# An attention and expert block on one core: the last sequence's experts computed densely, and score stacks of 128 rows

## The chip, the cores and the metric

The kernel runs on one core of a Trainium2 chip. The metric is device time in microseconds (us) of one execution. A core has a matrix engine (PE, with its weight loads as PEld), a vector engine (DVE), an activation engine (ACT), a general engine (POOL) and an engine that here only issues transfers (SP). Each works through its own queue of instructions in order and waits on semaphores for the others. SBUF is the on-chip memory of 128 partitions, PSUM the memory that PE writes to, DRAM the memory outside.

## What is computed

`x` is 8 sequences of 256 tokens with 128 channels, f32. Four residual steps follow each other, each on the LayerNorm of `x`:

```python
x = x + attn_a(layernorm(x))     # 16 heads of 8 channels; w_qkv and w_proj in 8 groups of 16 channels
x = x + ffn(layernorm(x))        # f = 0
x = x + attn_b(layernorm(x))     # 16 heads of 8; dense Wq, Wk, Wv, Wo; q and k RMS-normalised per head
x = x + ffn(layernorm(x))        # f = 1, the same weights as f = 0

def ffn(h):                      # 16 experts, each token goes to its best 4
    probs = softmax(h @ router_w + router_b)
    topw, topi = top_k(probs, 4)
    topw = topw / sum(topw)
    combine = sum(one_hot(topi, 16) * topw[..., None], axis=2)
    out = 0
    for e in range(16):          # 128 -> 256 -> 128
        hmid = gelu(h @ w1[e] + b1[e], approximate=False)
        out = out + (hmid @ w2[e] + b2[e]) * combine[:, e, None]
    return out
```

## The kernel before

**Tiles.** The 2048 tokens are 16 tiles of 128 (`NT`), two to a sequence, and two halves `hf` of 8 tiles (`TPH`). `x` stays in SBUF as `x_sb` for the whole kernel.

**Attention** (`attention`, scores in L734 to L758, weighing in L760 to L782). A sequence is four steps (`SEQ`); a step does four heads twice. q and k are split into three bf16 parts (`split2`, `split_cast`, `split3`, L502 to L529), written to DRAM (`qd`, `kd`) and read back by `stack_in` (L531 to L543) as stacks `qst` and `kst` of 128 partitions x 16 heads x 256 tokens, of which 72 rows are filled (R = 9 x 8: nine products of the parts). They come from a pool with two buffers per tag. One scores matmul (L745) takes 72 rows, 128 keys and 256 queries; ACT takes the exponential of 1024 columns at once (L754); the weighing of the values (L772) uses 32 columns of PE per head. The first sequence of attention a goes another way, in f32 (`project_1`, `scores_1`), with its `q1` and `k1` in the buffers of the stacks.

**Experts** (`routed`, `experts`, `fetched`). For each half, `route1` to `route3`, `chosen`, `rows_of` pick each token's 4 experts and give it a row in each expert's room of CAP = 320 rows; the row numbers come from a matmul in `route2`. `send` (L952) scatters each tile's rows into `sent[hf]` in DRAM: POOL issues 4 indirect DMAs per tile (L959). Then the 16 experts run in pairs, one expert a step: `load` (L1008) reads a pair's rows, `turn` (L1021) transposes them, `front` (L1037) does the first matmul into `ps_h` (L1045) and the gelu (L1053), `second` (L1061) the second into `ps_y` (L1068); DVE adds the bias into `ys` (L1075) and the ACT queue stores it to `made[hf]` (L1083). `fetch` (L1107) gathers each token's 4 results back, 4 indirect DMAs per tile on POOL (L1118); `combine` (L1125) adds them to `x_sb` with their weights (four DVE operations per tile, L1129) and, for f = 1, writes the tile out (L1136). The first two of a tile's 4 results (`EARLY`) are read from the rows of the first 14 experts alone, so that their gathers need not wait for the last pair; they are placed at the half's end - 0.5, the others at the end + 1.5. For the first half four tiles are fetched at first and the other four as buffers come free; in the last half of f = 1 all eight are fetched at once, into two tiles `yg4` in the buffers of `kst`.

**Order.** The order on PE, ACT, DVE and SP is written out by hand: main units (attention steps and expert steps) are numbered 0 to END - 1, each is a front and a back one step later, and every other piece is put at a place between them with `at(place, f)`. The places are the tables FINISH, ROUTE, PREPARE, COMBINE, PROJECT, TURN and BACK (L55 to L92), in steps from the sequence's or half's own step. `needs` and `done` check at build time that a piece stands behind what it builds on. POOL's order follows from the order in which the pieces are reached. The units run in this order:

```python
units = attention(0, wo_a, ga, 1, base[0])
for hf in range(NH):
    units += experts(0, hf, base[1] + hf * E)
units += attention(1, wo_b, gb, 3, base[2])
for hf in range(NH):
    units += experts(1, hf, base[3] + hf * E)
```

A buffer is reused when its last reader is done: PSUM has three buffers for transposes and small results (`ps_tr`), one for `ps_acc` (`ps_y` and `ps_av`) and two for the big ones (`ps_big`).

Of the kernel before, what the change touches and what calls it, by code (L numbers as in the profile page):

```python
# [40 lines left out]
P = 128  # L42
# [8 lines left out]

FINISH = [[[1.5, 1.7, 2.5, 3.5, 3.7], [-0.5, 0.1, 1.9, 2.9, 3.1], [0.7, 0.9, 2.1, 2.3, 2.3]],  # L55
          [[0.7, 2.1, 2.5, 3.9, 3.9], [0.3, 0.3, 2.7, 3.7, 3.7], [0.7, 0.9, 1.7, 2.7, 2.9]]]

ROUTE = [[[[4.7, 4.7, 5.7, 6.9, 6.9, 7.1, 7.7, 10.1], [5.5, 5.5, 6.5, 6.9, 6.9, 7.9, 7.9, 11.7],
           [4.5, 4.9, 4.9, 5.9, 6.1, 6.7, 6.7, 9.1]],
          [[5.3, 5.3, 5.9, 5.9, 5.9, 9.9, 9.9, 9.9], [6.7, 6.7, 7.7, 8.7, 8.9, 9.3, 9.3, 10.3],  # L60
           [4.1, 4.1, 5.1, 5.3, 5.3, 7.9, 8.3, 9.1], [3.5, 3.5, 4.5, 5.5, 5.7, 6.3, 6.3, 7.3]]],
         [[[4.3, 5.3, 6.5, 7.3, 7.5, 7.5, 7.5, 9.5], [4.5, 5.7, 6.1, 6.7, 6.7, 7.7, 7.9, 11.7],
           [4.3, 4.5, 5.5, 6.5, 6.7, 7.5, 7.7, 8.7]],
          [[5.5, 5.7, 6.5, 6.7, 7.7, 9.1, 9.3, 10.5], [4.5, 4.5, 5.5, 6.3, 6.3, 6.7, 6.7, 9.7],
           [4.5, 4.9, 5.5, 6.1, 6.1, 7.9, 7.9, 8.7], [3.1, 3.7, 4.7, 5.3, 6.1, 6.9, 7.1, 9.1]]]]

PREPARE = [[-7.97, -7.96, -7.95, -6.9, -5.9, -5.9, -5.9, -5.9, -3.9],
           [-11.5, -10.5, -9.5, -9.5, -7.9, -7.9, -7.9, -7.9, -6.9],
           [-11.1, -10.1, -9.1, -8.7, -7.7, -7.5, -6.3, -6.3, -6.3],
           [-12.5, -11.5, -10.5, -9.9, -7.7, -7.300000000000001, -5.5, -5.5, -4.5],  # L70
           [-11.7, -10.7, -9.7, -8.9, -7.9, -7.9, -7.9, -7.9, -6.9],
           [-13.3, -12.3, -11.3, -11.3, -9.9, -8.7, -7.9, -7.9, -6.5]]

COMBINE = [[[5.1, 5.5, 6.5, 7.5, 9.5, 11.5, 13.7, 15.5],
            [5.9, 5.9, 6.9, 7.9, 9.9, 12.1, 14.1, 16.1]],
           [[8.9, 6.9, 9.9, 11.9, 12.9, 14.9, 15.9, 17.9],
            [4.5, 5.5, 6.5, 6.5, 8.5, 11.5, 14.5, 15.5]]]

PROJECT = [[[6.7, 7.3, 8.1, 8.5, 9.3, 9.7, 9.7, 9.7, 11.1],
            [8.3, 9.3, 10.3, 11.1, 11.1, 12.1, 13.1, 13.1, 13.5],  # L80
            [13.1, 14.1, 15.1, 16.1, 16.1, 17.1, 18.1, 18.1, 19.1],
            [16.5, 18.7, 19.3, 19.3, 20.5, 21.3, 22.7, 22.7, 23.9]],
           [[6.3, 6.7, 8.5, 8.5, 10.1, 10.3, 11.3, 11.3, 11.7],
            [8.7, 9.5, 10.5, 10.5, 11.5, 12.5, 14.1, 14.1, 15.5],
            [13.5, 13.5, 14.5, 14.5, 15.5, 16.5, 17.5, 17.5, 18.5],
            [16.5, 17.5, 18.5, 18.5, 19.3, 20.9, 21.1, 21.1, 22.1]]]
# [9 lines left out]
def fast_path(  # L96
# [38 lines left out]
    RJ = CAP // HP  # L135
# [6 lines left out]
    LIMITS = [(E - 2) * CAP] * EARLY + [E * CAP] * (TOPK - EARLY)  # L142
# [150 lines left out]
    first_i = const.tile([P, E], I32, name="first_i")  # L293
    nc.gpsimd.iota(first_i, pattern=[[-CAP, E]], base=TOP, channel_multiplier=0)
    first = const.tile([P, E], F32, name="first")
    nc.gpsimd.tensor_copy(first, first_i)
# [7 lines left out]

    limit = const.tile([P, TOPK], F32, name="limit")
    for c, rows in enumerate(LIMITS):
        nc.gpsimd.memset(limit[:, c : c + 1], float(TOP - rows + 1))
# [4 lines left out]
    b2_bc = const.tile([P, NPAIR, C], F32, name="b2_bc")  # L312

# [39 lines left out]
    def load_b2():  # L353
        b2p = b2.rearrange("(r a) c -> a r c", a=2)
        for a in range(2):
            nc.sync.dma_start(
                b2_bc[a * HP : (a + 1) * HP], b2p[a : a + 1].to_broadcast((HP, NPAIR, C))
            )
# [105 lines left out]
    class Group:  # L464


        def __init__(self, t0, t1):
            self.t0, self.t1, self.n = t0, t1, t1 - t0
            self.step = None

# [21 lines left out]
    def ln_transpose(g, rows=None):  # L492
        pt = ps_tr("pt_h")
        for i in range(g.n):
            row = g.h[:, i, :] if rows is None else rows[:, g.t0 + i, :]
            nc.tensor.transpose(pt[:, i * P : (i + 1) * P], row, ident)  # L496
        hT = work.tile([P, g.n * P], F32, tag=f"hT{g.n}", name="hT")
        nc.scalar.copy(hT, pt[:, : g.n * P])  # L498
        g.hT = hT


# [29 lines left out]
    def stack_in(g, queue=nc.sync, parts=1, part=0):  # L531

        qd, kd = g.qkd
        if part == 0:
            g.qst = work.tile([P, H, N], BF16, tag="qst", name="qst")
            g.kst = work.tile([P, H, N], BF16, tag="kst", name="kst")
# [15 lines left out]
    def project_1(g):  # L552
# [4 lines left out]
        g.q1 = work.tile([P, NJ, N], F32, tag="qst", name="q1")  # L557
        g.k1 = work.tile([P, N], F32, tag="kst", name="k1")
# [4 lines left out]
    def heads_1(g, j0, j1):  # L563
        for j in range(j0, j1):
            nc.vector.tensor_scalar(g.q1[:, j, :], g.pq1, one_head[:, j : j + 1], None, ALU.mult)
# [127 lines left out]
    between = {}  # L693
    done = set()
# [9 lines left out]
    def attention(which, w_out, groups, k_next, base):  # L704
# [4 lines left out]
        def scores_1(n):  # L709
# [5 lines left out]
            for i in range(4):  # L715
# [3 lines left out]
                    g.q1[32 * i : 32 * i + 32, 2 * hf : 2 * hf + 2, :].rearrange("p j n -> p (j n)"),  # L719
# [14 lines left out]
        def scores(n):  # L734
# [4 lines left out]
            exs[n] = []  # L739
            for u in range(2):  # L740
                ps = ps_big("ps_st")
                for hh in range(2):
                    h = (hf * 4 + 2 * u + hh) * 2 + jj
                    for c in range(TB):
                        nc.tensor.matmul(  # L745
                            ps[:, hh, c * N : (c + 1) * N],
                            kst[0:R, h, c * P : (c + 1) * P],
                            qst[0:R, h, :],
# [146 lines left out]
    def route2(g, earlier, exps):  # L895
# [6 lines left out]
        g.exps = exps  # L902
        ps = ps_tr("ps_row")
# [16 lines left out]
    def rows_of(f, g):  # L920

        hf = g.t0 // TPH
        r3 = g.rows.rearrange("p (t e) -> p t e", e=E)
        here = work.tile([P, g.n, E], F32, tag=f"here{g.n}", name="here")
        nc.vector.scalar_tensor_tensor(here, r3, float(CAP), g.mb, ALU.is_lt, ALU.mult)
        key = work.tile([P, g.n, E], F32, tag=f"key{g.n}", name="key")
        nc.vector.tensor_tensor(
            key, first.unsqueeze(1).to_broadcast([P, g.n, E]), r3, ALU.subtract
# [12 lines left out]
        if g.t1 % TPH == 0:  # L941
            nc.vector.tensor_tensor(here, r3, g.mb, ALU.add)
            nc.vector.tensor_reduce(
                most[:, f * NH + hf : f * NH + hf + 1],
                here.rearrange("p t e -> p (t e)"),
                AX.X,
                ALU.max,
            )
# [24 lines left out]

    def route3(f, g):
# [4 lines left out]
            g.tk, g.tk, limit.unsqueeze(1).to_broadcast([P, g.n, TOPK]), ALU.max  # L979
        )  # L980
        if not g.exps:
            t = work.tile([P, g.n, E], F32, tag=f"exl1{g.n}", name="ex1", bufs=1)
            nc.vector.tensor_scalar(t, g.ex, -1.0, 1.0, ALU.mult, ALU.add)
            nc.vector.reciprocal(t, t)
            nc.vector.scalar_tensor_tensor(g.ex, g.ex, 1.0, t, ALU.add, ALU.mult)
# [17 lines left out]
    def experts(f, hf, base):  # L1003

        xs, hs, gs, ys = {}, {}, {}, {}
        JA = 3

        def load(r):  # L1008
            if r == 0:
                assert len(scattered[hf]) == TPH * TOPK  # L1010
            x = work.tile([P, RJ, C], F32, tag="xs", name="xs", bufs=3)
            ins = nc.sync.dma_start(
                x, sent[hf][r * 2 * CAP : (r + 1) * 2 * CAP].rearrange("(p j) c -> p j c", j=RJ)
# [7 lines left out]
        def turn(r, part):  # L1021
            if part == 0:
                hs[r] = work.tile([P, 2, RJ, HP], F32, tag="hs", name="hs")
# [13 lines left out]
        def front(e):  # L1037
# [5 lines left out]
            g = work.tile([P, NI, RJ, HP], F32, tag="ex", name="g", bufs=4)  # L1043
            for n in range(NI):
                nc.tensor.matmul(  # L1045
                    ps[:, n, :CAP],
                    w1_sb[r][:, a, n * P : (n + 1) * P],
                    hs[r][:, a].rearrange("p j q -> p (j q)"),
# [3 lines left out]
            for n in range(NI):  # L1052
                nc.scalar.activation(  # L1053
                    g[:, n].rearrange("p j q -> p (j q)"),
                    ps[:, n, :CAP],
# [5 lines left out]
        def second(r, j0, j1):  # L1061
            if j0 == 0:
                ys[r] = work.tile([P, RJ, C], F32, tag="ys", name="ys")
# [17 lines left out]
            if j1 == RJ:  # L1081
                del gs[2 * r], gs[2 * r + 1]
                nc.scalar.dma_start(  # L1083
                    made[hf][r * 2 * CAP : (r + 1) * 2 * CAP].rearrange("(p j) c -> p j c", j=RJ),
# [17 lines left out]

    yg = {}
# [3 lines left out]
    def fetch(f, t, c0, c1, last=False):  # L1107

        needs(("fetchable", f, t))
        if last:  # L1110
            i = t % 4
            if i == 0:
                many.append(work.tile([P, 4, TOPK, C], F32, tag="kst", name="yg4"))
# [3 lines left out]
        for c in range(c0, c1):  # L1117
# [3 lines left out]
                in_=made[t // TPH][0 : LIMITS[c]],  # L1121
# [18 lines left out]
    END = base[3] + NH * E  # L1140
# [14 lines left out]

# [734 lines left out]
```

## Time and profile before

| | us |
|---|---|
| runs | 683.42, 679.70, 676.77, 677.83; median 678.77 |
| profiled execution | 682.4, span 680.6, mean granted PE clock 0.787 |
| attention a, about | 0 to 150 |
| experts f = 0 | 150 to 312 |
| attention b | 312 to 490 |
| experts f = 1 | 490 to 634 |
| last gathers and combines | 634 to 680.6 |

| engine | busy us | share of the span |
|---|---|---|
| PE | 470.3 | 69% |
| ACT | 281.8 | 41% |
| DVE | 267.1 | 39% |
| POOL | 260.0 | 38% |

The profile is one execution. A group row reads: line, engine, operation, output<-input, shape and count, then busy time and mean ns of one, then the idle time of the engine just before these instructions and what ended most of it. "remote" or "another core or an unknown queue" is a wait whose end the profile could not tie to an instruction. The granted clock is the share of full speed that PE was given. In the page's slices each digit is a tenth of a slice of 17 us. A row of windows gives busy time and count of instructions of each engine in a stretch, then the clock, the busy share of the DMA engines and GB/s.

### The profile page before, as it was taken

Reading aid. Unit: us, or ns where it says so; the run is one execution under the profiler, and the core shown is the slowest. Engines: PE = TensorE matmul, PEld = TensorE weight load, DVE = VectorE, ACT = ScalarE, POOL = GpSimd, SP = SyncE. Lnnn points to the kernel's source line nnn. Section 1 sums busy time; section 2 is a strip of 40 time slices with the busy share of each in tenths; the row PEclk is TensorE's granted clock in tenths of the full one; section 3 lists DMA queues with packets and bytes.
Section 4 is the critical chain, followed back from the end, with each engine's and each line's share of the span. In section 5 each row is a group of like instructions: output and inputs, shape, how many; then the busy total and the mean of one; then the engine's idle time right before and its main releaser. Section 6 shows DMA issues by size and latency. Waiting matters only on the chain.

```text
span 680.6 us, 10365 instructions
## 1 busy us (share of the span) xinstructions
PE 470.3 (69%) x3739; PEld 297.2 (44%) x3739; DVE 267.1 (39%) x1086; ACT 281.8 (41%) x523; POOL 260.0 (38%) x303
## 2 busy tenths in 40 slices
PE   7799559788787938787673976786739795896100
PEld 3366334355455716454241553343527463564100
DVE  5346333335541103484172673442427311042323
ACT  5589325465232403355372762564613242342000
POOL 6100724404453263504444007053533506235674
PEclk9899865777787978798595877686859888697655
DMA  4777742745443423247164163352113233332322
GB/s 114 185 181 212 193 113 82 177 130 154 149 127 105 127 70 99 78 122 190 45 152 99 38 146 104 78 134 88 55 46 99 101 121 96 97 94 86 92 59 59
DMA packets 53283, 76.53 MB, mean 112 GB/s; under 512 B 9032, under 2 KB 36200, under 8 KB 51064
## 3 DMA queue, kind: packets, MB, share of 16 engines
q1 hardware_dynamic: 40104, 48.41, 26.9%
q0 software_dynamic: 8224, 16.86, 9.0%
q10 hardware_dynamic: 4896, 10.52, 4.1%
q8 instruction: 31, 0.51, 0.3%
q14 instruction: 28, 0.23, 0.1%
HBM read 42.73 MB, written 33.03 MB: 111 GB/s over the span
## 4 chain that ended last, share of the span: by engine, by line
PE 48%; another core or an unknown queue 19%; ACT 9%; DVE 8%; issue 8%; DMA 4%; POOL 2%; SPq 1%; DVEq 0%; ACTq 0%; POOLq 0%
PE ps_y L1068 11%; PE ps_h L1045 9%; PE ps_av L772 8%; PE ps_st L745 7%; ACT ex L754 5%; PE pt_x L1028 4%; PE pq L618 2%; DVE x_sb L1129 2%; POOL yg L1118 2%; DVE ys L1075 2%; PE pp L829 1%; PE ps_lg L860 1%; PE pt_o L790 1%; DMA kst<-kd 1%
## 5 line engine op out<-in xcount | busy, mean ns | idle before, releaser
L959 POOL DMA_INDIRECT sent<-h,dst x128 | 123.5, 965 | 199.8 <-DVE dst L938 95.9
L1118 POOL DMA_INDIRECT yg<-made,src x128 | 121.4, 949 | 163.5 <-issue 56.6
L754 ACT ACTIVATE ex<-ps_st 128x1024 f32<-128x1024 f32 x120 | 117.1, 1023 | 66.9 <-PE ps_st L745 35.5
L1068 PE MATMUL ps_y<-w_sb,g 128*64 128x128 f32 x1280 | 94.4, 299 | 48.6 <-DVE ys L1075 41.4
L1068 PEld LDWEIGHTS ps_y<-w_sb,g 128*64 128x64 f32 x1280 | 77.7, 150 | 80.3 <-DVE ys L1075 51.0
L772 PE MATMUL ps_av<-ex,vst 128*32 128x256 f32 x1024 | 96.9, 456 | 17.6 <-ACT av L782 8.5
L745 PE MATMUL ps_st<-qst,kst 72*128 72x256 bf16 x480 | 77.2, 309 | 30.8 <-issue 22.1
L1045 PE MATMUL ps_h<-hs,w_sb 128*128 128x320 f32 x256 | 96.3, 503 | 2.6 <-issue 1.9
L1075 DVE TENSOR_TENSOR ys<-ps_y,b_bc 128x384 f32<-128x384 f32 x64 | 31.4, 490 | 165.5 <-remote 69.2
L1053 ACT ACTIVATE g<-ps_h,b1T 128x320 f32<-128x320 f32 x128 | 60.7, 526 | 61.8 <-PE ps_h L1045 36.4
L745 PEld LDWEIGHTS <-kst 72*128 72x128 bf16 x480 | 51.5, 110 | 51.2 <-issue 39.4
L1029 ACT COPY hs<-pt_x 128x384 f32<-128x384 f32 x64 | 26.9, 427 | 100.7 <-PE pt_x L1028 23.4
L1045 PEld LDWEIGHTS ps_h<-hs,w_sb 128*128 128x128 f32 x256 | 50.9, 221 | 18.4 <-issue 9.8
L772 PEld LDWEIGHTS ps_av<-ex,vst 128*32 128x32 f32 x1024 | 32.1, 122 | 60.4 <-issue 42.1
L1129 DVE SCALAR_TENSOR_TENSOR x_sb<-yg,wgt,x_sb 128x128 f32<-128x128 f32 x128 | 44.3, 352 | 30.7 <-DMA yg<-made,src 23.3
L1028 PE MATMUL pt_x<-ident,xs 128*128 128x128 f32 x160 | 33.6, 316 | 2.2 <-issue 2.2
L841 DVE TENSOR_TENSOR x_sb<-pp,x_sb 128x256 f32<-128x256 f32 x16 | 6.8, 422 | 51.5 <-remote 30.8
L498 ACT COPY hT<-pt_h 128x256 f32<-128x256 f32 (+1 forms) x30 | 11.7, 388 | 36.2 <-PE pt_h L496 14.9
L600 POOL TENSOR_TENSOR x_sb<-x_sb,bp_bc 128x256 f32<-128x256 f32 x8 | 6.2, 778 | 49.0 <-DVE h L483 49.0
L1028 PEld LDWEIGHTS pt_x<-ident,xs 128*128 128x128 f32 x160 | 19.9, 156 | 10.8 <-issue 9.9
L790 PE MATMUL pt_o<-ident,av 128*128 128x128 f32 x64 | 13.1, 339 | 12.5 <-ACT av L782 12.5
L860 PE MATMUL ps_lg<-rw_sb,hT 128*128 128x16 f32 x64 | 11.8, 306 | 13.3 <-ACT hT L498 9.8
(159 smaller groups left out, 464.9 us busy)
## 6 DMA issues: line engine op xcount, KB each, us to landing
xs<-sent SPq DMA_DIRECT2D x32, 320.0 KB
made<-ys ACTq DMA_DIRECT2D x32, 320.0 KB
qst<-qd SPq DMA_DIRECT2D x45, 192.0 KB
kst<-kd SPq DMA_DIRECT2D x45, 192.0 KB
sent<-zero SPq DMA_DIRECT2D x20, 256.0 KB
w_sb<-in_L_ffn_w_dram SPq DMA_DIRECT2D x16, 256.0 KB
qd<-qk_parts SPq DMA_DIRECT2D x15, 192.0 KB
kd<-qk_parts SPq DMA_DIRECT2D x15, 192.0 KB
```

Of the source, the lines that this page charges most:

```text
L745: nc.tensor.matmul(ps[:, hh, c * N : (c + 1) * N], kst[0:R, h, c * P : (c + 1) * P], qst[0:R, h, :], start=True, stop=True,)
L754: nc.scalar.activation(ex, ps.rearrange("p h (c n) -> p h c n", c=TB), AF.Exp, scale=SCALE)
L772: nc.tensor.matmul(acc[32 * i : 32 * i + 32, hf * N : (hf + 1) * N], groups[b].v[:, c, v0 : v0 + W], ex[i // 2][:, i % 2, m, :], start=(jj ...
L959: ins = nc.gpsimd.indirect_dma_start(out=sent[hf], out_offset=bass.IndirectOffsetOnAxis(ap=dst[:, g.t0 + i, c : c + 1], axis=0), in_=g.h[: ...
L1028: nc.tensor.transpose(pt[:, (j - j0) * P : (j - j0 + 1) * P], x[:, j, :], ident)
L1029: nc.scalar.copy(hs[r][:, :, j0:j1, :], pt[:, : (j1 - j0) * P].rearrange("p (j a q) -> p a j q", a=2, q=HP),)
L1045: nc.tensor.matmul(ps[:, n, :CAP], w1_sb[r][:, a, n * P : (n + 1) * P], hs[r][:, a].rearrange("p j q -> p (j q)"), start=True, stop=True,)
L1053: nc.scalar.activation(g[:, n].rearrange("p j q -> p (j q)"), ps[:, n, :CAP], AF.Gelu, bias=b1T[:, e * NI + n : e * NI + n + 1],)
L1068: nc.tensor.matmul(acc[a * HP : (a + 1) * HP, (j - j0) * C : (j - j0 + 1) * C], gs[2 * r + a][:, n, j, :], w2_sb[r][:, a, n, :], start=(n ...
L1075: nc.vector.tensor_tensor(ys[r][:, j0:j1, :], acc[:, : (j1 - j0) * C].rearrange("p (j c) -> p j c", c=C), b2_bc[:, r, :].unsqueeze(1).to_b ...
L1118: nc.gpsimd.indirect_dma_start(out=yg[t][:, c, :], out_offset=None, in_=made[t // TPH][0 : LIMITS[c]], in_offset=bass.IndirectOffsetOnAxis ...
L1129: nc.vector.scalar_tensor_tensor(x, y[:, c, :], wgt[:, t, c : c + 1], x, ALU.mult, ALU.add)
```

## The change

1. In f = 1, the last sequence (two tiles) is neither sent nor gathered. Its routing stops after the choice of the experts; `weights_of_all` makes a weight for each of the 16 experts (zero for those not chosen). Sixteen steps behind the sparse ones (`all_experts`) run each expert on all 256 tokens of the sequence, and DVE adds each result to `x_sb` with its column of weights; the biases come in with one small matmul. POOL then issues 8 scatters and 8 gathers fewer, and the last half has CAP3 = 256 rows per expert and 6 tiles.
2. The stacks `qst` and `kst` are four fixed tiles in two pairs, used in turn. POOL clears their rows 64 to 127 at the start, and scores matmuls go over all 128 rows; the rows behind the 72 are zero. `q1` and `k1` of the first sequence lie in the room of the first expert weights, and the last gathers in the two tiles `qst`.
3. The tables of places are new, FINISH, ROUTE, PREPARE, COMBINE and PROJECT; of them the diff below shows parts.

The diff, cut to its core:

```diff
+CAP3 = 256
...
-          [[5.5, 5.7, 6.5, 6.7, 7.7, 9.1, 9.3, 10.5], [4.5, 4.5, 5.5, 6.3, 6.3, 6.7, 6.7, 9.7],
-           [4.5, 4.9, 5.5, 6.1, 6.1, 7.9, 7.9, 8.7], [3.1, 3.7, 4.7, 5.3, 6.1, 6.9, 7.1, 9.1]]]]
+          [[5.5, 5.7, 6.5, 6.7, 7.7, 9.1, 9.3, 10.5], [4.5, 4.5, 5.5, 6.3, 6.3, 6.7, 7.7, 10.7],
+           [4.5, 4.9, 5.5, 8.1, 8.1, 9.9, 9.9, 10.7], [5.1, 5.7, 6.7, 8.7, 8.7, 8.7, 8.7, 9.1]]]]
...
-COMBINE = [[[5.1, 5.5, 6.5, 7.5, 9.5, 11.5, 13.7, 15.5],
+COMBINE = [[[5.1, 5.3, 6.5, 6.5, 9.5, 11.5, 13.7, 15.5],
             [5.9, 5.9, 6.9, 7.9, 9.9, 12.1, 14.1, 16.1]],
-           [[8.9, 6.9, 9.9, 11.9, 12.9, 14.9, 15.9, 17.9],
-            [4.5, 5.5, 6.5, 6.5, 8.5, 11.5, 14.5, 15.5]]]
+           [[8.9, 6.9, 10.9, 13.1, 13.9, 15.9, 16.9, 18.9], [11.1, 12.1, 12.5, 12.1, 13.1, 13.5]]]
...
-    LIMITS = [(E - 2) * CAP] * EARLY + [E * CAP] * (TOPK - EARLY)
+
+    def limits(cap):
+        return [(E - 2) * cap] * EARLY + [E * cap] * (TOPK - EARLY)
+
+
+    SENT = ((TPH, TPH), (TPH, TPH - TB))
...
+    stacks, n_stack = [], [0]
+    for i in range(2):
+        q_k = [const.tile([P, H, N], BF16, name=f"{n}st{i}") for n in "qk"]
+        for st in q_k:
+            nc.gpsimd.memset(st[HP:P], 0.0)
+        stacks.append(q_k)
...
-            g.qst = work.tile([P, H, N], BF16, tag="qst", name="qst")
-            g.kst = work.tile([P, H, N], BF16, tag="kst", name="kst")
+            g.qst, g.kst = stacks[n_stack[0] % 2]
+            n_stack[0] += 1
+            if n_stack[0] > 2:
+                needs(("scored", n_stack[0] - 2))
...
-        g.q1 = work.tile([P, NJ, N], F32, tag="qst", name="q1")
-        g.k1 = work.tile([P, N], F32, tag="kst", name="k1")
+
+        g.q1 = w1_sb[:2]
+        g.k1 = w1_sb[2][:, 0, :]
...
+            if n % SEQ == SEQ - 1:
+                n_scored[0] += 1
+                done.add(("scored", n_scored[0]))
...
-                            kst[0:R, h, c * P : (c + 1) * P],
-                            qst[0:R, h, :],
+                            kst[:, h, c * P : (c + 1) * P],
+                            qst[:, h, :],
...
+        if g.all:
+            return
...
-            x = work.tile([P, RJ, C], F32, tag="xs", name="xs", bufs=3)
+                assert len(scattered[hf]) == SENT[f][hf] * TOPK
+            x = work.tile([P, MJ, C], F32, tag="xs", name="xs", bufs=3)[:, :RJ, :]
...
-                    ps[:, n, :CAP],
+                    ps[:, n, :cap],
...
+    def weights_of_all(g):
+
+        w = work.tile([P, g.n, E], F32, tag="wall", name="w_all", bufs=1)
+        if not g.exps:
+            plain_exp(g)
+        nc.vector.tensor_tensor(w, g.ex, g.mb, ALU.mult)
+        sm = work.tile([P, g.n, 1], F32, tag=f"sm{g.n}", name="sm")
+        nc.vector.tensor_reduce(sm, w, AX.X, ALU.add)
+        nc.vector.reciprocal(sm, sm)
+        nc.vector.tensor_tensor(w, w, sm.to_broadcast([P, g.n, E]), ALU.mult)
+        g.w = w
...
+    def all_experts():
+
+        gs, wTs = {}, []
...
+        def front(e):
+            g = whole[0]
+            ps = ps_big("ps_h")
+            x = work.tile([P, NI, g.n * P], F32, tag="ex", name="g", bufs=4)
+            for n in range(NI):
+                nc.tensor.matmul(
+                    ps[:, n, : g.n * P],
+                    w1_sb[e // 2][:, e % 2, n * P : (n + 1) * P],
+                    g.hT,
+                    start=True,
+                    stop=True,
+                )
+            for n in range(NI):
+                nc.scalar.activation(
+                    x[:, n, :],
+                    ps[:, n, : g.n * P],
+                    AF.Gelu,
+                    bias=b1T[:, e * NI + n : e * NI + n + 1],
+                )
+            gs[e] = x
+
+        def back(e):
+            g = whole[0]
+            ps = ps_tr("ps_y")
+            x = gs.pop(e)
+            for i in range(g.n):
+                for n in range(NI):
+                    nc.tensor.matmul(
+                        ps[:, i * C : (i + 1) * C],
+                        x[:, n, i * P : (i + 1) * P],
+                        w2_sb[e // 2][:, e % 2, n, :],
+                        start=(n == 0),
+                        stop=(n == NI - 1),
+                    )
+            for i in range(g.n):
+                xs = x_sb[:, g.t0 + i, :]
+                nc.vector.scalar_tensor_tensor(
+                    xs, ps[:, i * C : (i + 1) * C], g.w[:, i, e : e + 1], xs, ALU.mult, ALU.add
+                )
+            if e == 0:
+                transpose_w()
+            elif e == 1:
+                biases(wTs.pop())
+            elif e == E - 1:
+                nc.sync.dma_start(of[:, g.t0 : g.t1, :], x_sb[:, g.t0 : g.t1, :])
...
-                many.append(work.tile([P, 4, TOPK, C], F32, tag="kst", name="yg4"))
+                rows = stacks[len(many)][0].rearrange("p h n -> p (h n)").bitcast(F32)
+                many.append(rows.rearrange("p (t k c) -> p t k c", t=4, k=TOPK))
...
-                in_=made[t // TPH][0 : LIMITS[c]],
+                in_=made[t // TPH][0 : limits(CAPS[f][t // TPH])[c]],
...
-    END = base[3] + NH * E
+    END = base[3] + NH * E + E
...
+                g.all = (f, g.t1) == (1, NT)
...
+                if g.all:
+                    at(n[7], weights_of_all, g)
+                    whole.append(g)
+                    continue
...
-            ts = [hf * TPH + i for i in range(TPH)]
+            ts = [hf * TPH + i for i in range(SENT[f][hf])]
...
-            n = TPH if last else 4
+            n = len(ts) if last else 4
...
+    units += all_experts()
```

## The prediction

> **What bounds the kernel now.** I read the page's slices and chain first, then the waits and the timeline of one stretch where the chain names no engine, then tables of windows. From the page (busy tenths in 40 slices of 17 us; then the chain of waits):
>
> ```profile
> PE   7799559788787938787673976786739795896100
> POOL 6100724404453263504444007053533506235674
> PEclk9899865777787978798595877686859888697655
> ...
> PE 48%; another core or an unknown queue 19%; ACT 9%; DVE 8%; issue 8%; DMA 4%; POOL 2%; SPq 1%; DVEq 0%; ACTq 0%; POOLq 0%
> L959 POOL DMA_INDIRECT sent<-h,dst x128 | 123.5, 965 | 199.8 <-DVE dst L938 95.9
> L1118 POOL DMA_INDIRECT yg<-made,src x128 | 121.4, 949 | 163.5 <-issue 56.6
> L745 PE MATMUL ps_st<-qst,kst 72*128 72x256 bf16 x480 | 77.2, 309 | 30.8 <-issue 22.1
> L1075 DVE TENSOR_TENSOR ys<-ps_y,b_bc 128x384 f32<-128x384 f32 x64 | 31.4, 490 | 165.5 <-remote 69.2
> ```
>
> PE is the bound for nine tenths of the span and stands still in the last three slices, where POOL works alone. Only one core runs, so the 19% (127 us) that the chain gives to "another core" are something else. The timeline of the 16 gathers at 563.7 shows what:
>
> ```profile
> 577.51 0.94 POOL L1118 DMA_INDIRECT yg<-made,src  x1 [0.30 <-issue]
> 577.92 0.56 DVE L1075 TENSOR_TENSOR ys<-ps_y,b_bc 128x384 f32<-128x384 f32 x1 [10.80 <-remote]
> 578.54 1.58 PEld L1068 LDWEIGHTS ps_y<-w_sb,g 128*64 128x64 f32 x16 [7.82 <-DVE ys L1075]
> 578.54 1.98 PE L1068 MATMUL ps_y<-w_sb,g 128*64 128x128 f32 x16 [7.31 <-DVE ys L1075]
> ...
> 585.65 0.95 ACT L1053 ACTIVATE g<-ps_h,b1T 128x320 f32<-128x320 f32 x2 [4.54 <-remote]
> 586.50 0.42 DVE L1075 TENSOR_TENSOR ys<-ps_y,b_bc 128x256 f32<-128x256 f32 x1 [8.02 <-remote]
> ```
>
> DVE and ACT wait 10.80, 8.02 and 4.54 us for matmuls that PE had ended; PE then stops for want of PSUM. It happens wherever POOL issues 8 or more indirect DMAs in a row, so I read it as: PE's completions reach the others late while such a burst runs. How much work passes, and what the clock does, is in the table of windows (PE, its weight loads, DVE, ACT, POOL, clock, DMA):
>
> ```profile
> 40.00:60.00 20.00, 20.00 (x218) 13.49 (x220) 10.45 (x42) 18.81 (x29) 1.46 (x2) 1.00 0.77 197
> 100.00:120.00 20.00, 18.34 (x117) 9.93 (x118) 8.10 (x42) 9.62 (x14) 7.96 (x8) 0.50 0.32 98
> 563.70:583.50 19.80, 11.97 (x84) 7.95 (x81) 2.72 (x11) 3.12 (x7) 15.19 (x16) 0.77 0.37 98
> 583.50:603.50 20.00, 16.68 (x145) 12.28 (x146) 4.26 (x10) 8.41 (x19) 2.07 (x3) 0.80 0.27 93
> 633.30:673.00 39.70, 0.36 (x8) 0.11 (x3) 12.71 (x39) 0.00 (x0) 30.25 (x32) 0.53 0.28 75
> ```
>
> 84 matmuls pass in the burst, 145 in the same time after it. In the last row the 32 gathers of the second half's 8 tiles run 39.7 us, 1.24 us each, beside an idle PE.
>
> **Part by part, against the profiled run's 682.4 us** (span 680.6, and 1.8 around it; that run lies 3.6 above the median of 678.8, within the runs shown).
>
> *128-row stacks: −8.* More rows should not lengthen a matmul: at full clock 8 of L745 (72 rows, 256 columns, bf16) take 0.88 us, 0.11 each, and 4 of L571 (128 rows, 256 columns, f32) 0.86, 0.215 each, so f32 costs two such passes and the rows nothing. What can change is the clock. Between 100 and 120 PE is busy 18.34 of 20 us and yet at 0.50, so busy time is not what keeps it at 1.00. The granted clock changes only at a grid of 3.4 us. I weighed each matmul of the trace by its active rows/128 and columns/128 and summed by grid window: of 82 windows under 0.35, one was followed by full clock; of 119 above, 115 were. Scores at 72 rows weigh 0.56, the 32-column weighing of the values 0.25, so a half-clock attention stage sits just under the line and stays there; at 128 rows it weighs some 0.5. Eight windows would flip (31.8, one of 72.8 to 79.6, four of 103.5 to 117.1, 376.6, one of 397 to 407). If PE's time in them halved it would be 8 × 1.7 = 13.6; ACT's exponentials (1.02 us each, up to 18.81 of 20 us) take part of it: 8, bounds 0 and 13. That zeros count is seen at the start: the warm-up matmuls on a zero tile alone hold the clock at 1.0.
>
> The Trainium skill ("TensorE: Matmul & The Clock Gate", Part 1, The HAM clock gate) has the gate follow how busy PE was in the last 3.4 us window. By that rule, zeros behind the 72 rows buy nothing and this term is 0; the 100 to 120 row speaks against it.
>
> Rows 64 to 127 of four tiles are cleared by POOL at the start. The nearest rows: 128x1088 f32 in 1.00 us, 128x512 in 0.53; a 64x4096 bf16 clear is then 2 to 3.9 us, four 8 to 16, behind the POOL work that ends at 9.5 us. The first stack DMAs go at about 20, the first add of the bias (L600, 0.78 us) is needed at about 38; 0, and up to +4 if the first third rows are late. The first sequence's q1/k1 move to w1_sb, whose loads start at 141.7, so nothing queues behind them on SP. The new wait of a stack on the scores two sequences back stands where the two-buffer tag waited already: 0.
>
> *Last sequence neither sent nor gathered: −5.* Its 8 scatters run 533.9 to 543.7; in 530 to 548 PE waits 5.8 us for DVE at L1068 and DVE 7.3 for "remote". Behind that is only PE's own work; bounds 0 and −8.
>
> *Second half at 256 rows per expert: −7.* Each pair loses a fifth: L1045 4 matmuls 1.08 → 0.86 us twice, L1068 24+16 → 16+16 (1.46+1.02 → 2.04), turns 5 → 4 × 0.16. Sum 5.5 → 4.5, × 8 = 8. The gathers of the first half (16, still in one burst) fall into it and cost what they cost: 7, bounds 5 and 8. Its late gathers and combines come one step apart later and nearer to the combines that free their buffers (the bursts at 600.8 and 608.7 stall PE up to 8.6 us): −3, bounds 0 and −5.
>
> *The end: +10.* Before, the early gathers start at T0 = 633.3 (pair 6 is stored), PE's last matmuls end at 633.7, and the span ends at T0+47.3: 39.7 of gathers, 2.7 of combine, 4.9 for the out DMA. After, gathers are 24 × 1.24 = 29.8. Beside them lie 16 dense steps: PE 4 records of 256 columns (0.86) and 8 of 128 (0.14 each, from L829) = 1.96 us, say 2.15 with the gaps seen in the expert stage; ACT 2 gelus 0.82, DVE 2 × 0.35. Undisturbed that is 16 × 2.15 + 0.6 + 4.9 = T0+40, −7. But this is PE work in a burst longer than any that the trace shows with PE busy. By the 84 matmuls in 19.8 us, 126 pass in 29.8, 10 of the 16 steps. By the stops (two or three tiles deep, then 8 to 11 us of waiting) 5. I take 7: burst, 2.8 us until all is released (16 sends end at 89.0, DVE goes on at 91.8), 9 × 2.15, 5.5: T0+57.6, +10. Bounds −8 and +18 (3 steps in the burst, rest begun at half clock).
>
> *New places: 0 beyond these*: each queue keeps its kind of work; bounds ±3.
>
> Sum: −8−5−7−3+10 = −13: 669.4, or **666 us** beside the median.
>
> **Rivals.** *A, the burst stops the dense work, slower (0.22).* The early 12 gathers catch the last expert pair, whose store the late 12 await. T0+15 end of the first, +2.8 release, +5.6 for the pair's last matmuls, ys and store (3.4 us from ys to the gather at 563.70), +15: T0+38, release at 41, 15 steps × 2.15, 3.4 of half clock, 5.5: T0+82, +35. Sum 694.4, 691 by the median. It decides when fewer than four of 16 steps are done by then. For it: in the 16 sends at 69.0 DVE got nothing for 16.4 us. Against: gathers released twice in 20 us, and in before the last pair ended 0.4 us into its burst without a stop.
> *B, dense steps run freely (0.17).* Tail −7, sum 652: 649. Against: every burst of 8 or more.
> *C, the zero rows do not move the clock (0.19)*, so the change does not do what its stacks are for: 677.4, 674.
>
> **Numbers.** My forecast has 0.42: 659 to 676. The range 647 to 688 leaves out half of B and the upper part of A. A measurement here tells about 1% from no change: faster than 672 is most of the forecast, B and a third of C, 0.63; within 1% is half of C and a quarter of A, 0.18; slower is most of A and a little of C, 0.19.
>
> **What would show it.** Clock 1.00 in most of attention (mean 0.787 → above 0.83); no stall near 535; the second half some 10 us shorter; after it a burst of about 30 us with "remote" waits of 5 to 12 us on DVE and ACT, some 80 to 130 matmuls in it, and dense steps 2.1 us apart behind. Wrong if the dense steps go at an even pace beside POOL, if 0.50 stays between 100 and 120, or if the stacks' DMAs wait for POOL at 20.

## The result, and the profile after

The changed kernel takes 683.26 us (median of 34 runs, 674.15 to 694.88), the kernel before 678.47 in the same measurements (55 runs, 670.72 to 687.75). The ratio is 1.0053, 95% interval 1.0030 to 1.0077: a small loss. (Ratios here and below are taken over the runs of each kernel that lie within 1.5% of its fastest, so they are not the quotient of the two medians.) The prediction was 666, a gain; 683 lies inside its range of 647 to 688, but on the other side of no change. The profiled execution took 676.83 us, span 675.1, below its own median.

The page of the changed kernel, the lines that answer to those of before (slices of 17 us; then groups: line, engine, operation, count | busy us, mean ns | idle before, and what ended most of it). The page follows no chain of waits for this profile.

```profile
PE   6699647598786847598482875766568983969274
POOL 9500544404543355303535017241713135336710
PEclk9799859788777959599785998796769796979768
...
L988 POOL DMA_INDIRECT sent<-h,dst x120 | 115.3, 961 | 185.3 <-DVE rden L832 48.3
L773 PE MATMUL ps_st<-qst,kst 128*128 128x256 bf16 x480 | 71.8, 292 | 39.1 <-ACT ex L782 18.1
L1113 DVE TENSOR_TENSOR ys<-ps_y,b_bc 128x384 f32<-128x384 f32 (+1 forms) x64 | 30.3, 473 | 160.0 <-remote 64.0
L1246 POOL DMA_INDIRECT qst<-made,src x24 | 22.8, 950 | 10.1 <-issue 7.9
```

PE now works to the end (last slice 4 instead of 0), the scores are shorter (292 against 309 ns; the clock is higher), and the waits marked "remote" are still there. The table of windows, with the stretch that stood at half clock before, then the last burst and the time behind it (PE, its weight loads, DVE, ACT, POOL, clock, DMA):

```profile
100.00:120.00 20.00, 13.81 (x146) 8.10 (x139) 8.79 (x47) 8.70 (x15) 7.68 (x8) 0.93 0.61 166
618.00:645.20 27.20, 11.22 (x64) 9.63 (x62) 5.18 (x17) 3.66 (x9) 20.78 (x22) 0.79 0.22 57
645.20:670.00 24.80, 20.40 (x112) 18.27 (x112) 14.00 (x46) 7.95 (x20) 0.01 (x1) 0.82 0.07 19
```

Between 100 and 120 the clock went from 0.50 to 0.93, though PE is busy less (13.81 against 18.34 us). In the burst of 22 gathers only 64 matmuls pass in 27.2 us; 80 to 130 were expected.

**A second kind of chip.** The 18 experiments ran on three chips, and on two of them (numbers 3 and 4) the kernel before takes 489 to 492 us where it takes 679 on the third (15). I call the third, and those of the first measurements, late, and the two others prompt, by what the waits show. The waits of the kernel before on chip 3 (us in total, times, longest):

```profile
DVE ys L1075 <- PE ps_y L1068: 76.2, 47, 3.9
POOL x_sb L600 <- DVE h L483: 47.4, 6, 13.1
```

There is no "remote" among the long ones; on the late chips L1075 alone had 69.2 us of it. POOL's operations last the same (968 and 965 ns a scatter). So the stops by POOL's bursts come with some chips, not with the program alone, and every comparison below is within one kind.

Stages, from the first matmul of each (`ps_h` of the experts, the last sparse `ps_y`), in us. The one late profile of before is a run 3.9 us above the median of 678.47, so the late differences are uncertain by about that much. "After, late" is the mean of five profiles (the changed kernel twice and three experiments that differ only behind the last burst's start; the row to the end is of the two alone), "before, prompt" the mean of four:

| stage | before, late (one profile) | after, late | forecast | measured | before, prompt | after, prompt | measured |
|---|---|---|---|---|---|---|---|
| start to second experts (f = 1) | 486.7 | 484.3 | −8 | −2.4 | 351.0 | 341.6 | −9.4 |
| its first half | 73.4 | 66.6 | −5 | −6.8 | 46.4 | 45.9 | −0.5 |
| its second half | 73.3 | 69.2 | −10 | −4.1 | 48.2 | 41.2 | −7.0 |
| from there to the end | 47.2 | 61.0 | +10 | +13.8 | 46.7 | 41.0 | −5.7 |
| span | 680.6 | 681.1 | −13 | +0.5 | 492.2 | 469.7 | −22.5 |

### The profile page after: what moved, and what is told of

It reads as the page before. It is cut to its first block, busy times and chain, and to the rows that moved or that the text cites. A ratio compares the mean times of both kernels' runs of the same rounds, so it can differ in the third digit from the quotient of the medians.

```text
span 675.1 us, 10673 instructions
## 1 busy us (share of the span) xinstructions
PE 474.9 (70%) x3857; PEld 316.5 (47%) x3857; DVE 276.1 (41%) x1102; ACT 290.8 (43%) x555; POOL 258.4 (38%) x297
## 4 chain that ended last, share of the span: by engine, by line
## 5 line engine op out<-in xcount | busy, mean ns | idle before, releaser
L1246 POOL DMA_INDIRECT yg<-made,src x96 | 91.1, 949 | 151.9 <-DVE x_sb L1257 51.0
L1106 PE MATMUL ps_y<-w_sb,g 128*64 128x128 f32 x1216 | 91.9, 303 | 52.1 <-DVE ys L1113 36.0
L773 PE MATMUL ps_st<-qst,kst 128*128 128x256 bf16 x480 | 71.8, 292 | 39.1 <-ACT ex L782 18.1
L1113 DVE TENSOR_TENSOR ys<-ps_y,b_bc 128x384 f32<-128x384 f32 (+1 forms) x64 | 30.3, 473 | 160.0 <-remote 64.0
L1083 PE MATMUL ps_h<-hs,w_sb 128*128 128x320 f32 (+1 forms) x256 | 89.8, 475 | 3.3 <-issue 2.4
L1091 ACT ACTIVATE g<-ps_h,b1T 128x320 f32<-128x320 f32 (+1 forms) x128 | 58.8, 511 | 51.9 <-PE ps_h L1083 31.4
L773 PEld LDWEIGHTS <-kst 128*128 128x128 bf16 x480 | 48.5, 104 | 58.5 <-issue 49.8
L1067 ACT COPY hs<-pt_x 128x384 f32<-128x384 f32 (+1 forms) x64 | 26.0, 414 | 102.9 <-remote 39.3
L1193 PE MATMUL ps_y<-w_sb,g 128*128 128x128 f32 x128 | 20.3, 311 | 16.7 <-issue 16.2
L1193 PEld LDWEIGHTS ps_y<-w_sb,g 128*128 128x128 f32 x128 | 19.5, 222 | 19.1 <-issue 17.0
L1246 POOL DMA_INDIRECT qst<-made,src x24 | 22.8, 950 | 10.1 <-issue 7.9
```

The costliest lines, as they stand in the source:

```text
L773: nc.tensor.matmul(ps[:, hh, c * N : (c + 1) * N], kst[:, h, c * P : (c + 1) * P], qst[:, h, :], start=True, stop=True,)
L1083: nc.tensor.matmul(ps[:, n, :cap], w1_sb[r][:, a, n * P : (n + 1) * P], hs[r][:, a, :RJ].rearrange("p j q -> p (j q)"), start=True, stop=True,
L1091: nc.scalar.activation(g[:, n, :RJ].rearrange("p j q -> p (j q)"), ps[:, n, :cap], AF.Gelu, bias=b1T[:, e * NI + n : e * NI + n + 1],)
L1106: nc.tensor.matmul(acc[a * HP : (a + 1) * HP, (j - j0) * C : (j - j0 + 1) * C], gs[2 * r + a][:, n, j, :], w2_sb[r][:, a, n, :], start=(n ...
L1113: nc.vector.tensor_tensor(ys[r][:, j0:j1, :], acc[:, : (j1 - j0) * C].rearrange("p (j c) -> p j c", c=C), b2_bc[:, r, :].unsqueeze(1).to_b ...
L1193: nc.tensor.matmul(ps[:, i * C : (i + 1) * C], x[:, n, i * P : (i + 1) * P], w2_sb[e // 2][:, e % 2, n, :], start=(n == 0), stop=(n == NI ...
```

## The experiments

All times in this section are medians, ratios are to the kernel before on the same chip, with 95% intervals. The repeats of the kernel before are single profiled runs and have no interval.

**1. The kernel before again, and the whole change again.** No edit. `before_again`, `before_third`, `before_fourth` and `before_fifth` were meant as further sets of stage times; all four met prompt chips.

> The unchanged kernel once more, for a second set of stage times. If its first profile (span 680.6, clock 0.787) was an ordinary one, attention a ends near 152, the first experts near 308, attention b near 487 and the last gathers start near 633, each within 2 us, with a clock of 0.78 to 0.79. If that profile was an unlucky one (it lay 3.6 us above the median), attention, where PE sits at the edge of half clock, is some 4 to 6 us shorter here and the clock 0.80 or more.

> The unchanged kernel, for stage times beside the five profiles of the changed one. With late completions (a time near 680): if attention's share of my sum was right, attention a to the first experts' start at 152 to 154, the first experts 156 to 160 long, attention b 176 to 179, the rest 192 to 195. If the profile of before was an unlucky one in attention: attention a and b together 6 us shorter than there (330.4), and the stacks' true gain is about 0. Without late completions (a time near 490): the stage times of the second profile again, within 3 us.

> The unchanged kernel for stage times where completions are late. If my attention term was right: attention a and b near 152 and 178 us, second experts' start near 487, last part 192 to 195. If the first profile was an unlucky one in attention: second experts' start at 480 to 484, so that the changed kernel's 484 (mean of five profiles) is no gain at all. Without late completions: 131, 232, 349, 490 as before, within 3.

> The unchanged kernel for stage times. With late completions: if my attention term was right, second experts' start near 487 and the last part 192 to 195; if the first profile was an unlucky one in attention, start at 480 to 484. Without: 131, 232, 349, 490 again, within 3.

Measured: spans 489.7, 492.1, 491.5 and 495.4, clocks 0.889 to 0.898; their mean is in the table. A second set of stage times of the kernel before on a late chip was not got.

> The changed kernel once more with the others of this call. The two kernels were timed near 680 where PE's completions reach DVE and ACT late during POOL's bursts (remote waits in the profile); the first four experiments ran on a chip where such waits are missing and the kernel before takes 489. With late completions: 1.003 to 1.008 against before, last burst to end of the span 55 to 61 us. Without them: 0.955 to 0.970 against before, dense steps at an even 1.5 to 1.8 us and the end some 40 us after the last experts.

> The changed kernel. Without late completions it has not been run yet: small clears gave 0.948 and 72 rows 0.962, so with the long clears 0.953 to 0.960, the dense steps at an even 1.5 to 1.8 us beside the gathers, and the end some 36 to 40 us after the last experts: the same code is a gain of 4 to 5% there. With late completions: 1.003 to 1.008, a sixth profile.

Measured: late 682.21, 1.0043 (1.0011 to 1.0076); prompt 468.97, 0.9544 (0.9485 to 0.9603). The same code loses half a per cent on one kind of chip and gains 4.6% on the other. On the late chip the mean clock of the kernel before was 0.798 over 17 runs, that of the changed one 0.832 over 12. Part of this is the end, where PE now works: in the late profiles the clock up to the second experts is 0.796 before and 0.827 to 0.849 after.

**2. The end: dense steps without the gathers, gathers without the dense steps.**

The first leaves out the last half's experts from its six tiles:

```diff
+            if last:
+                for i, t in enumerate(ts):
+                    at(end + COMBINE[f][hf][i], write_out, t)
+                continue
```

The second leaves out the experts of the last sequence:

```diff
-        return [(lambda e=e: front(e), lambda e=e: back(e)) for e in range(E)]
+        return [(lambda: None, lambda e=e: out_only(e)) for e in range(E)]
```

> The changed kernel without the last half's 24 gathers and their combines (its six tiles go out without those experts). With late completions: if the burst stops the dense steps (my step, +10 at the end), the last expert pair to the end falls from about 58 to 36 to 40 us, some 20 less than the changed kernel. Rival (the dense steps are slow by themselves): it stays above 50. Without late completions: within 5 us of the changed kernel.

> The changed kernel without the 16 dense steps (the last sequence goes out without its experts). Burst 24 x 1.24 = 29.8 and some 7 to 9 behind: 37 to 39 us from the first gather to the end on either kind of chip. With late completions that is some 20 us under the changed kernel, so neither part alone makes its end long; without, 0 to 5 us under it.

Measured, late chip: 659.12, 0.9723 (0.9668 to 0.9777), and 664.50, 0.9792 (0.9736 to 0.9847). From the last sparse matmul to the end: 34.9 and 38.2 us; together in the two late profiles of the changed kernel 60.5 and 61.6. Each part alone is short, so on this chip it is their meeting that costs. The same stretch of 27.2 us in windows, of the dense steps alone (late chip):

```profile
618.00:645.20 27.20, 27.20 (x189) 25.20 (x186) 13.46 (x43) 11.77 (x29) 0.00 (x0) 1.00 0.11 32
```

189 matmuls at full clock, against 64 at 0.79 beside the burst. On a prompt chip, in a stretch of the same length beside 23 gathers, 168 pass:

```profile
433.00:460.20 27.20, 24.70 (x168) 22.89 (x168) 14.48 (x47) 10.92 (x26) 20.50 (x23) 1.00 0.23 65
```

The timeline of the changed kernel on the late chip shows the waits (idle time before, and its end, in brackets):

```profile
624.72 1.03 PE L1171 MATMUL ps_h<-hT,w_sb 128*128 128x256 f32 x4
626.53 0.61 DVE L1202 SCALAR_TENSOR_TENSOR x_sb<-ps_y,w_all,x_sb 128x128 f32<-128x128 f32 x2 [3.09 <-PE ps_h L1171]
630.13 0.84 ACT L1179 ACTIVATE g<-ps_h,b1T 128x256 f32<-128x256 f32 x2 [6.93 <-remote]
637.12 0.61 DVE L1202 SCALAR_TENSOR_TENSOR x_sb<-ps_y,w_all,x_sb 128x128 f32<-128x128 f32 x2 [9.98 <-remote]
644.88 0.84 ACT L1179 ACTIVATE g<-ps_h,b1T 128x256 f32<-128x256 f32 x2 [13.92 <-remote]
645.41 2.07 PE L1193 MATMUL ps_y<-w_sb,g 128*128 128x128 f32 x8 [11.28 <-issue]
649.07 1.13 DVE L1202 SCALAR_TENSOR_TENSOR x_sb<-ps_y,w_all,x_sb 128x128 f32<-128x128 f32 x4 [11.34 <-remote]
```

By the burst's end at 645.2 DVE has added up five dense steps (those at 626.53 and 637.12 are the fourth and fifth), and the release comes 3.9 us behind it. The activation at 644.88 reads the matmuls of 624.72, which PE's row has ended at 625.75, 19 us earlier. In the other direction the wait is short: PE goes on at 645.41, 0.5 us after ACT does. So what is late goes from PE to the others, as far as a profile tells that only models the ends of matmuls.

The same place on a prompt chip, in the changed kernel: gathers at the same 1.25 us, and the steps 1.76 us apart beside them, with no "remote".

```profile
437.52 0.94 POOL L1246 DMA_INDIRECT qst<-made,src  x1 [0.31 <-PE ps_y L1193]
437.95 1.05 PE L1193 MATMUL ps_y<-w_sb,g 128*128 128x128 f32 x8
438.21 0.84 ACT L1179 ACTIVATE g<-ps_h,b1T 128x256 f32<-128x256 f32 x2 [0.92 <-PE ps_h L1171]
438.77 0.94 POOL L1246 DMA_INDIRECT qst<-made,src  x1 [0.30 <-issue]
439.71 1.05 PE L1193 MATMUL ps_y<-w_sb,g 128*128 128x128 f32 x8
```

**3. The gathers in groups.** Each tile's four gathers wait for a dense step's sum, so that POOL pauses.

```diff
+BEHIND = (0, 3, 5, 8, 10, 13)
+    def fetch_behind(f, t, e):
+        for ins in fetch(f, t, 0, TOPK, True):
+            after(ins, dense[-1:])
...
+            if last:
+                for i, (t, e) in enumerate(zip(ts, BEHIND, strict=True)):
+                    at(end + e + 0.1, fetch_behind, f, t, e)
+                    at(end + e + 5.1, combine, t, k_next)
+                continue
```

> The changed kernel with the last gathers in six groups of four, a tile each, and each group waiting on POOL for a dense step's sum, so that POOL pauses between groups. With late completions: if it is a long unbroken burst that holds completions back, stops of at most 5 us that PE's buffers mostly cover, the end some 46 us after the last experts, 10 to 14 us less than the changed kernel (0.985 against before). Rival (every gather holds back completions for its own time, broken or not): no gain, or a loss up to 10 us. Without late completions: 2 to 6 us more than the changed kernel, as the last gathers come later.

Measured, late chip: 668.12, 0.9828 (0.9780 to 0.9876), against 1.0043 for the changed kernel: 14 us less, and faster than both kernels. The last sparse matmul to the end took 52.1 us in its profile, 9 us less than in the changed kernel, in a run 5.9 us above its own median. Where the rest of the 14 was gained no profile shows. The timeline shows POOL's pause, and stops of ACT of 4.80 to 5.57 us, where the changed kernel's profile had 6.93 and 13.92:

```profile
626.68 0.94 POOL L1256 DMA_INDIRECT qst<-made,src  x1 [4.35 <-issue]
...
635.27 0.84 ACT L1181 ACTIVATE g<-ps_h,b1T 128x256 f32<-128x256 f32 x2 [4.80 <-remote]
```

The groups did not stay apart as I meant: they ran as bursts of 2, 10, 8 and 4, so there may be more to be had.

**4. The start: the clears in pieces.** The profiles of the changed kernel showed a second sequence that began its exponentials at 33.8 instead of 29.9. DVE's normalisation beside the clears, in the kernel before and the changed one:

```profile
10.31 0.60 DVE L483 TENSOR_SCALAR h<-x_sb,mv,rstd 128x128 f32<-128x128 f32 x2
19.32 0.60 DVE L483 TENSOR_SCALAR h<-x_sb,mv,rstd 128x128 f32<-128x128 f32 x2
```

```profile
9.59 3.51 POOL L520 MEMSET qst<- 64x4096 bf16 x1
10.23 3.01 DVE L495 TENSOR_SCALAR h<-x_sb,mv,rstd 128x128 f32<-128x128 f32 x2
...
20.31 3.51 POOL L520 MEMSET kst<- 64x4096 bf16 x1
21.06 2.90 DVE L495 TENSOR_SCALAR h<-x_sb,mv,rstd 128x128 f32<-128x128 f32 x2
```

Each pair begins within a clear and ends as the clear ends. What reads PSUM beside them is not slowed (L620: 0.41 us at 13.16, 0.43 in the kernel before).

```diff
-            nc.gpsimd.memset(st[HP:P], 0.0)
+            for j in range(0, H, 2):
+                nc.gpsimd.memset(st[HP:P, j : j + 2], 0.0)
```

> The changed kernel with the four clears of 3.51 us each cut in eight. In the changed kernel's profile DVE's normalisation (L495, SBUF to SBUF) takes 3.01 and 2.90 us beside a clear, 0.60 without, and the second sequence's exponentials start at 33.8 instead of 29.9. If the long clears hold DVE: both at 0.6 to 1.1 us, the second sequence at 29.5 to 31, some 3 us less in the time: with late completions 0.997 to 1.001 against before (the changed kernel 1.0043), without 0.958 to 0.965. Rival (the start waits for something else, as the stack loads behind the clears): the second sequence stays at 33 or later.

Measured, prompt chip: 463.69, 0.9478 (0.9433 to 0.9524), against 0.9544 of the changed kernel; the second sequence starts at 30.2. The two ratios come from different chips and their intervals overlap, so the gain in time is not settled. The start is: in all 13 profiles with the long clears the second sequence starts at 33.2 to 34.7, in the two with the small ones at 29.9 and 30.2, and the rows show why:

```profile
10.23 0.89 DVE L495 TENSOR_SCALAR h<-x_sb,mv,rstd 128x128 f32<-128x128 f32 x2
18.91 0.76 DVE L495 TENSOR_SCALAR h<-x_sb,mv,rstd 128x128 f32<-128x128 f32 x2
```

The Trainium skill ("SBUF — State Buffer", Who interferes with whom) says that DVE's tensor_scalar can enter a mode in which it contends with POOL for a shared pair of ports, and that whichever issues first holds the pair for its whole instruction. This fits 3.01 beside 3.51 us, and 0.89 beside pieces of an eighth; that L495 ran in that mode no row shows. I had not weighed it. On a late chip the small clears were not run.

**5. Both cures.** The groups and the small clears together.

> Both cures together: the last gathers in groups of four behind dense steps, and the clears in eight pieces each. With late completions: the groups gave 0.9828, the clears should take 3 to 4 us more off: 0.976 to 0.980. If the start's delay is made good later on anyway: 0.982. Without late completions: the groups cost 2 to 6 us there, so 0.952 to 0.962, against 0.948 for the small clears alone.

Measured, prompt chip: 462.48, 0.9507 (0.9463 to 0.9552), not to be told from the small clears alone: where completions are prompt the groups cost nothing that shows. On a late chip it was not run.

**6. The stacks alone, and the change without them.** The kernel before with only the fixed stacks and their clears (four stack loads up to one step later, which the fixed tiles ask for); and the changed kernel over 72 rows:

```diff
-                            kst[:, h, c * P : (c + 1) * P],
-                            qst[:, h, :],
+                            kst[0:R, h, c * P : (c + 1) * P],
+                            qst[0:R, h, :],
```

> The kernel before with only the fixed stacks of 128 rows (and four stack loads up to one step later, which the fixed tiles ask for). My step (zero rows lift the clock, 8 us): ratio about 0.988, mean clock above 0.81, attention a and b together 6 to 10 us shorter. Rival 1 (the clock rises, but ACT's exponentials or the stops by POOL's bursts hold the time): clock above 0.81, ratio 0.995 to 1.003. Rival 2 (zeros do not count): clock 0.78 to 0.79, ratio 1.000.

> The kernel before with the fixed stacks alone, where completions are late (the earlier run met a chip without them and gave 1.0018 at a clock of 0.927 against 0.907). With late completions: my step less the clears, 8 - 4 = 4 us: 0.994, clock 0.82 to 0.83. Rival (time in attention is set by the stops and by ACT, not by PE's rate): 1.000 to 1.006, the 4 us of the clears and nothing for them. The rest of the span (from the second experts' start) within 2 us of the kernel before, 192 to 196.

> The stacks alone, where completions are late. My step less the clears, 8 - 4 = 4 us: 0.994, clock 0.82 to 0.83 against 0.80. Rival (the clock rises, the time does not, as on the other chips): 1.000 to 1.006. Last part (second experts' start to the end) 192 to 196, as in the kernel before. Without late completions: 1.000 to 1.002 for the third time.

> The stacks alone. With late completions: my step less the clears 0.994 at a clock of 0.82 to 0.83; rival (clock rises, time does not) 1.000 to 1.006. Without late completions: 1.000 to 1.007 as in the three earlier runs.

> The changed kernel with its scores over 72 rows as before. My step: slower than the changed kernel by 8 us, so some 1.017 against the kernel before, with a clock back under 0.80 in attention. Rival 1 (clock moves, time does not): 1.003 to 1.008 with the lower clock. Rival 2: no change in clock or time. The dense steps behind are the same in all three: the last burst starts and the span ends 55 to 60 us apart.

Measured, all on prompt chips: the stacks alone four times 1.0018 (0.9982 to 1.0053), 1.0006 (0.9959 to 1.0053), 1.0073 (1.0027 to 1.0119) and 1.0012 (0.9965 to 1.0059), at a mean clock of 0.925 to 0.928 against 0.904 to 0.908; 72 rows 0.9622 (0.9560 to 0.9684) at 0.958, against 0.9544 at 0.968. Attention a, 28 to 128 us, of the kernel before and of the stacks alone (chip 3):

```profile
28.00:128.00 100.00, 90.86 (x824) 56.68 (x825) 48.83 (x218) 69.46 (x106) 35.09 (x37) 0.85 0.71 195
```

```profile
28.00:128.00 100.00, 86.02 (x858) 55.19 (x861) 51.28 (x228) 72.39 (x111) 34.98 (x37) 0.95 0.78 203
```

These are one profile of four each. Over the four, the clock here is 0.80 to 0.86 in the kernel before and 0.87 to 0.95 with the stacks, with PE less busy (86 to 87 against 89 to 91 us); the four later loads are in this difference too.

What speaks for the zeros themselves is the prediction's own weighing, done again on the 14 profiles with 128 rows: each matmul by its time at full clock (0.11 us for 256 bf16 columns, twice that for f32), its active rows/128 and columns/128, summed by window of 3.4 us, against the clock of the next window. With the zero rows counted, a line at 0.38 has 52 of 2239 windows on the wrong side; with 72 rows counted the best line has 92, and the best line by PE's busy time alone 142. So the zeros count, rival 2 is out, and the rule of busyness sorts the windows worse.

The time is another matter: alone, the stacks lose about 4 us at the start and gain no more than that back. With the new places even the clock hardly needs the zeros: in the same 100 us it is 0.98 at 72 rows and 0.97 at 128. The two ratios are 0.0078 apart, some 4 us for the 128 rows, but the intervals overlap and the medians of the two calls, 468.36 and 468.97, do not show it: not settled. On a late chip the stacks were not run alone.

**7. The old places.** All tables as before wherever both kernels have them, with the same four loads later.

> The changed kernel with the places of before wherever both have them (four stack loads stay later, as the fixed tiles ask for). My step (places worth 0, the spaced gathers of the first half 3): within 3 us of the changed kernel, 1.000 to 1.010 against before. Rival (the new places are what costs the time in attention or in the experts): 0.985 to 0.995, with the stages before the last burst some 8 us shorter than in the changed kernel. Other rival (they are a real part of the gain): 1.015 or more.

> The changed kernel with the old places, where completions are late (the earlier run, on a chip without them, gave 0.9726). If the new places cost what the first experts lost (about 3 us, 156 before and 159 to 161 after): 0.999 against before. If they are worth 0 as I had it: 1.004. If they gain as they did there (0.9622 with the new places and 72 rows): 1.010 or more.

Measured, prompt chips: 476.14, 0.9726 (0.9668 to 0.9785), and 475.72, 0.9733 (0.9685 to 0.9781). The new places are worth about 1.8% there, some 9 us by the ratios and 7 by the medians (468.97 with them); I had them at 0, with bounds of 3 each way. On a late chip it was not run.

## Why the prediction was wrong

Against the profiled run of before (680.6), −13 was forecast and +0.5 came, and another 4 us lie in the base. By its steps:

- *The base.* I took the profiled run's 3.6 us above the median for something that both kernels have, and took it off the result. The mean of the changed kernel's stages (681.1 and 1.8 around) falls on its own median of 683.26, and the profiled run of before lies 1.7% above the fastest of its 55 runs (670.72), so the excess belonged to that one run: 4 us. In which stage it sat is open.
- *The clears at 0.* The bounds, 0 and +4, held the cost, but the value taken failed, and the cover named was the wrong one: I looked at who waits for POOL (the stack loads, the bias) and not at what else POOL's long instruction holds up. 3.51 us each, as bounded; DVE stood behind two of them. The second sequence starts 33.9 against 29.9 on the late chips: +4.0.
- *The clock, −8.* That zero rows count for the clock was right: by the weighing of experiment 6, 3 to 8 windows in each late profile lie above the line only through them, where eight were to flip. What they are worth in time is not shown. From the second sequence's start to the second experts the late chips show 456.8 before and 450.4 after, −6.4, close to −8, but the new places are in it and one profile of before stands behind it. On prompt chips the stacks alone gained no more than the 4 us that they cost, and the places alone some 7 to 9. So a hit here may be luck, and how the −6.4 is shared is open.
- *The scatters left out, −5.* −6.8 on the late chips, −0.5 on the prompt ones: as argued, this was a stop and not work.
- *The second half, −10 (7 and 3).* This is the largest miss: −4.1. PE's own work did fall as summed, 7.0 us on the prompt chips where nothing else binds. On the late ones the gathers of the first half still fall into the stage, unchanged, and hold DVE as long for less work (its waits marked "remote" at `ys`, L1113, are 25.5 us in this stage, 27.0 before); I had written that they "cost what they cost" and yet booked nearly the whole. Of the 3 for the spaced gathers nothing is seen: PE still stops for up to 9.0 us. That the bursts take what is missing is inferred from the two kinds of chip; no run took them away.
- *The end, +10.* +13.8. The step was "I take 7" dense steps in the burst; five were done by its end, and the other eleven came 2.0 us apart, as worked out. Undisturbed I had T0+40; the gathers alone took 38.2 and the dense steps alone 34.9, so the meeting costs some 23 us, where my sum had 17.6 (57.6 less 40). Rival A's stop of the last expert pair did not come; rival B is what prompt chips do (41.0).

The errors add up: 4.0 + 1.6 − 1.8 + 5.9 + 3.8 = 13.5, and about 4 in the base: from −12.5 beside the median to +4.8.

## What to carry to other kernels

A long burst of transfers may hold up engines that share no data with it, on some chips and not on others: before work is moved beside a burst, count how much passes in one that the trace shows, and break the burst. A single profile of the kernel before is one draw: its distance from the median is not common to both kernels. An instruction that "nobody waits for" is still to be asked what else cannot run while it does.

## What the runs showed of the hardware

Chips differ in how late DVE and ACT go on behind PE's matmuls during POOL's indirect DMAs: 679 and 489 to 492 us for one program, with waits up to 16.4 us marked "remote" on the one kind and none such on the other, at equal POOL durations (965 and 968 ns a scatter). Why, no run tells. The granted clock follows the rows and columns in use, zeros included: weighed so, 52 of 2239 windows of 3.4 us are sorted wrongly, 142 by busy time. With 56 rows of zeros the clock in attention a was 0.87 to 0.95 instead of 0.80 to 0.86. A DVE tensor_scalar pair of 0.60 us took 3.01 beside a POOL clear of 3.51, 0.89 beside clears of an eighth.
